# Keeping four groups' hidden layer of an FFN in SBUF, in a two-layer diffusion block on one core

## The chip, the cores and the metric

One NeuronCore of a Trainium2 chip runs the whole kernel as one program. The metric is the device time of one execution in microseconds, lower is better. Engines: PE (matrix multiply), DVE (vector), ACT (scalar and activation functions), POOL (GpSimd), SP (which here only issues DMAs).

## The reference

The input x has 128 sequences of 64 tokens of 256 features, 8192 tokens in all; cond is 128 x 256. Two layers each add to x:

```
hs = scan over 64 steps: gate = sigmoid(h @ Wh.T + z_t @ Wz.T + b); h = tanh(h*(1-alpha) + gate*z_t)   # z = x
xq = fake_quant(hs)                                  # one scale for the whole tensor, 8 bit
h  = silu(xq @ w_gate.T) * (xq @ w_up.T)             # 704 wide, quantised weights
x  = x + fake_quant(h) @ w_down.T                    # its scale needs max|h| over ALL tokens

# layer 1: adaptive layer norm, hyperbolic maps, attention of 16 heads inside each sequence, then an MLP
x2 = mobius_add(x, expmap(g_msa * attention(norm(x) * (1+sc_msa) + sh_msa)))
c  = mobius_add(x2, expmap(g_mlp * mlp(norm(x2) * (1+sc_mlp) + sh_mlp)))
out = x + fp6_block_quant(c) @ quantised(weight).T + bias
```

The maximum over all of h must be known before a single h can be quantised. So h has to be kept from the stage that makes it to the stage that uses it.

## The kernel before

The tokens stand as 64 tiles of 128 tokens, four tiles (512 tokens) to a group, 16 groups. The kernel has three stages.

**Scan** (until about 200 us). The 64 steps run one after another, with weight preparation in the gaps. `hsT` holds all steps in SBUF.

**h stage** (about 200 to 297 us). `hsT` is scaled to 8 bits into `xqT` in 16 blocks of 8 sequences (L493 to L507). Then for each group `tb`, `h_chunk` makes five tiles of h, 128 x 512 each; every second group adds a sixth tile with the last 64 columns of two groups. Each tile goes through ACT (silu), DVE or POOL (product `hv`), DVE (its maximum `am`), and a DMA stores it to DRAM (`h_d`, `hr_d`). At the end the maximum over everything gives the scale `cu`.

**Fused stage** (`fused`, from about 300 us). A loop over k from -5 to 18 runs a software pipeline. In iteration k stand, in program order:

- `tail(k)`: the Möbius sum of group k after attention, and of group k-3 after its MLP;
- `norms(k, ...)`: norm coefficients, `modulate`, the squares `un` of the norms, `su` from them, and the clip with `su`, for the MLP of group k and the attention of group k+5 together;
- `fp6(k-3)`: block quantisation, last matmul and the store of the result;
- `mlp(k)`, which ends in `tail_sums`;
- `attention(k+5)` in two pairs of tiles: `uT`, `qk`, `sq`, `nh`, `rh`, `comb`, `kT`, `e`, `raw`, the product into `u` (L1000), squares `tn`, `full`, `oT`, `av` (L1025), and then `tail_sums`;
- `front(k+6)`: loads h in pairs (`load_h`, `hl`), scales it to 8 bits with `cu` (`hb`, POOL), turns it to bf16 (`hq`), multiplies by `w_down` (`dn`), adds x (`xr`) and makes the statistics.

Iterations -5 to -1 have only attention work, 11 to 15 only the MLP, 16 to 18 only the last parts.

Sums of squares go through `square_sum`. ACT squares a tile into a scratch that nobody reads, and the accumulated sum is what counts. The scratch has one buffer for each tag, and the tag is made from the purpose and the engine: `u0`, `u1` for the norms (sums `un`), `o` for attention (`tn`), `ta`, `tm` for the tails (`ag`):

```
    def square_sum(e, tag, src, acc):

        junk = pl.tile([P, D], BF16, name="junk", tag=f"junk{tag}{e}", bufs=1)
```

Who is ahead of whom on an engine is decided when the program is built: a list scheduler takes the instructions by priority (program order, some chains raised by `first`), under the data dependencies and the order in which each tag's buffers are handed out. On the chip each engine executes its list in order. SBUF pools are stacks on the left and the right side; a tile of a pool that stands where another pool stood waits for the readers of that one.

Of the kernel before, what the change touches and what calls it, by code (L numbers as in the profile page):

```python
# [11 lines left out]
F32 = mybir.dt.float32  # L12
F32R = mybir.dt.float32r
BF16 = mybir.dt.bfloat16
I8 = mybir.dt.int8
F8 = mybir.dt.float8e4
# [6 lines left out]
P = 128  # L23
B, T, D = 128, 64, 256
# [17 lines left out]
GN = 4 * P  # L42
NG = NT // GN
AR = 8
TS = 4
CFG = {'rnd': 'S', 'ef': 8, 'fill': {'x1a': 'V', 'mod0': 'V'}, 'hold': [3, 0], 'mk': 2, 'raw': 1, 'mv': 6, 'xs': 3, 'la': 3, 'sb': 7, 'qks': 'GGGG', 'deq': 'VV', 'first': 1000, 'hb': 2, 'q_h': 'P', 'q_x1': 'P', 'q_xr': 'P', 'q_ot': 'P', 'q_out': 'P', 'q_ada': 'P', 'room': [[0.3, 0.3, 0.55], [0.5, 0.4, 0.2]], 'qv': 64, 'p1': 'GVGVGVGV', 'x1': 3, 'u1': 16, 'u2': 6, 'qkv': 2, 'sq': 1, 'uT1': 2, 'uT2': 2, 'qM': 2, 'kT': 2, 'e': 4, 'oT': 1, 'yT': 1, 'hq': 2, 'hl': 2, 'xr': 1, 'ot': 2, 'ada00': 2, 'ada02': 2, 'ada10': 2, 'ada12': 4, 'dn': 1, 'qk': 2, 'sc': 2, 'ao': 1, 'ml': 1, 'fp': 1, 'mod0': 'GGGV', 'mod1': 'VVVV', 'sqm0': 'SSSS', 'sqm1': 'SSSS', 'su0': 'VVVV', 'su1': 'VGVG', 'q8': 'GGGGGG', 'hqc': 'SSSVVV', 'qm': 'SSSS', 'x1a': 'GV', 'gate0': 'GGGG', 'gate1': 'GGGG', 'yb': 'GG', 'va': 'GGGG', 'sqt': 'SSSS', 'sqg': 'SSSS', 'sqo': 'SSVS', 'f2e': 'SSSS', 'early': 0, 'q8f': 'VVVVVV', 'hqf': 'SSSVVV', 'fl': 1, 'un': 2, 'jsu': 1, 'LA': 5, 'LM': 3, 'tl': 6, 'ord': 1, 'xt': 3, 'q_xt': 'P'}
GT = 4
NGR = NTILE // GT

LA, LM = CFG["LA"], CFG["LM"]  # L50
# [20 lines left out]
def tile_kernel(ctx, tc, a, out):  # L71
    nc = tc.nc
    V, S, G_, PE = nc.vector, nc.scalar, nc.gpsimd, nc.tensor
    dma = nc.sync.dma_start
# [65 lines left out]


    with ExitStack() as l0:
        fpool = l0.enter_context(tc.tile_pool(name="ffn0", bufs=1, side="right"))
        wgT = fpool.tile([P, 2, IF], BF16, name="wgT")
        wuT = fpool.tile([P, 2, IF], BF16, name="wuT")
        s_g = fpool.tile([P, 6], F32, name="s_g")
# [343 lines left out]
        fw = l0.enter_context(tc.tile_pool(name="fw", bufs=3))  # L490
        xp = hs_.enter_context(tc.tile_pool(name="xp", bufs=3))
        NBB = 8
        for b0 in range(0, B, NBB):  # L493
            for c in range(2):

                q8 = xp.tile([P, NBB, T], I8, name="q8", tag="q8")
                src = hsT[:, c, :, b0 : b0 + NBB].rearrange("p t b -> p b t")
                if b0 < CFG["qv"]:
                    V.tensor_scalar(q8, src, isx, None, ALU.mult)
                else:  # L500
                    G_.tensor_scalar(q8, src, isx, 0.0, ALU.mult, ALU.add)
                q8f = q8.rearrange("p b t -> p (b t)")
                dst = xqT[:, c, b0 * T : (b0 + NBB) * T]
                if c == 0:
                    V.tensor_copy(dst, q8f)
                else:
                    S.copy(dst, q8f)  # L507
        hs_.close()


        ps_a = l0.enter_context(tc.tile_pool(name="ps_a", bufs=3, space=PSUM))
# [1 line left out]

        cnt, silu = [0], []

        def h_chunk(pg, pu, j, at, dst):
            sil = fw.tile([P, GN], F32, name="sil", tag="sil")
            silu.append(S.activation(sil, pg, AF.Silu, scale=sgx[:, j : j + 1]))
            hv = fw.tile([P, GN], F32, name="hv", tag="hv", bufs=6)
            cnt[0] += 1  # L520
            if CFG["p1"][cnt[0] % 8] == "G":
                uv = fw.tile([P, GN], F32, name="uv", tag="uv")
                S.activation(uv, pu, AF.Copy, scale=sux[:, j : j + 1])
                G_.tensor_tensor(hv, uv, sil, ALU.mult)
            else:
                V.scalar_tensor_tensor(hv, pu, sux[:, j : j + 1], sil, ALU.mult, ALU.mult)  # L526
            V.tensor_reduce(am[:, j, at : at + 1], hv, AX.X, ALU.max, apply_absolute_value=True)  # L527
            dma(out=dst, in_=hv)

        V.memset(am, 0.0)  # L530
        for tb in range(NG):
            sl = slice(tb * GN, (tb + 1) * GN)
            for j in range(5):
                pg = ps_a.tile([P, GN], F32, name="pgate", tag="pgate")
                pu = ps_a.tile([P, GN], F32, name="pup", tag="pup")
                for ps, w in ((pg, wgT), (pu, wuT)):
                    for c in range(2):
                        PE.matmul(ps, lhsT=w[:, c, j * P : (j + 1) * P], rhs=xqT[:, c, sl],
                                  start=(c == 0), stop=(c == 1))
                h_chunk(pg, pu, j, tb, h_d[tb, j])  # L540
            if tb % 2:

                pg = ps_a.tile([P, GN], F32, name="pgate", tag="pgate")
                pu = ps_a.tile([P, GN], F32, name="pup", tag="pup")
                for ps, w in ((pg, wgT), (pu, wuT)):
                    for c in range(2):
                        for q in range(2):
                            s2 = slice((tb - 1 + q) * GN, (tb + q) * GN)
                            PE.matmul(ps[q * 64 : (q + 1) * 64], lhsT=w[:, c, 640:IF], rhs=xqT[:, c, s2],
                                      start=(c == 0), stop=(c == 1))  # L550
                h_chunk(pg, pu, 5, tb, hr_d[tb // 2])
        V.tensor_reduce(am1[:, 0:1], am, AX.XY, ALU.max)
        pmax(fpool, ps_t, am1[:, 1:2], am1[:, 0:1])
        sh = fpool.tile([P, 1], F32, name="sh")
# [7 lines left out]
def fused(ctx, tc, a, out_tok, x_tok, L):  # L562
# [8 lines left out]
    ada_d, h_d, hr_d, x1_d = (L[k] for k in ("ada_d", "h_d", "hr_d", "x1_d"))  # L571
    mx_scale, mx_round, ep, vas = (L[k] for k in ("mx_scale", "mx_round", "ep", "vas"))

    pl = ctx.enter_context(tc.tile_pool(name="fp", bufs=2))
    ps = ctx.enter_context(tc.tile_pool(name="fps", bufs=1, space=PSUM))
    one = ones[:, 0:1]
    len_pow = 4 * GT
# [10 lines left out]
    at = [0]  # L588
# [22 lines left out]
        return ps.tile([P, 512], F32, name=tag, tag=tag, bufs=CFG[tag])  # L611

    def big(tag, shape, dt=F32):
        return pl.tile(shape, dt, name=tag, tag=tag, bufs=CFG[tag])

    def square_sum(e, tag, src, acc):

        junk = pl.tile([P, D], BF16, name="junk", tag=f"junk{tag}{e}", bufs=1)
        if e == "S":
            S.activation(junk, src, AF.Square, accum_out=acc)  # L620
        else:
            V.scalar_tensor_tensor(junk, src, 1.0, src, ALU.mult, ALU.mult, accum_out=acc)

    def scale(e, dst, src, by):

        if e == "S":
            S.activation(dst, src, AF.Copy, scale=by)  # L627
        elif e == "V":
            V.tensor_scalar(dst, src, by, None, ALU.mult)  # L629
        else:  # L630
            G_.tensor_scalar(dst, src, by, 0.0, ALU.mult, ALU.add)  # L631
# [230 lines left out]

    def front(i):

        i0 = at[0] = i * GT
        x1 = x1s[i] = Pairs("x1")
        mv1 = get_mv(i - LA)[:, HA, :]
        for h2 in pairs:
            pr = i0 // 2 + h2
            early = pr < CFG["early"]  # L870
            grp = pr // 2
            hs_ = slice((grp % 2) * 64, (grp % 2) * 64 + 64)
            hl = hls.pop(0)
            hq = big("hq", [P, 6, 2 * P], BF16)
            q8 = big("hb", [P, 6, 2 * P], I8)

            for e, r, j in runs("q8f" if early else "q8", hs_):
                scale(e, q8[r, j, :], hl[r, j, :], cu[r])
            for e, r, j in runs("hqf" if early else "hqc", hs_):
                if e == "V":  # L880
                    V.tensor_copy(hq[r, j, :], q8[r, j, :])
                else:
                    S.copy(hq[r, j, :], q8[r, j, :])
            load_h(pr + CFG["hl"])
            xr = big("xr", [P, 2, D])
            move("xr", out=xr, in_=x_tok[:, i0 + 2 * h2 : i0 + 2 * h2 + 2, :])
            py = bank("dn")

            for i, j in [(i, j) for i in range(2) for j in range(5)] + [(0, 5), (1, 5)]:
                r = slice(0, P) if j < 5 else hs_  # L890
                PE.matmul(py[:, i * D : (i + 1) * D], lhsT=hq[r, j, i * P : (i + 1) * P], rhs=wdT[r, j, :],  # L891
                          start=(i == 0 and j == 0), stop=(j == 5), skip_group_check=True)
            V.tensor_tensor(x1.t[h2], two(py), bc_out(sdh, 2), ALU.mult)  # L893
            ENG[pick("x1a", h2)].tensor_tensor(x1.t[h2], x1.t[h2], xr, ALU.add)
            for g in (2 * h2, 2 * h2 + 1):
                stats(mv1[:, g, :], x1[g], 1)
            move("x1", out=x1_d[:, i0 + 2 * h2 : i0 + 2 * h2 + 2, :], in_=x1.t[h2])
# [172 lines left out]
    def fp6(i, av, s2):  # L1070
# [4 lines left out]
        for h2 in pairs:  # L1075
# [8 lines left out]
            V.reciprocal(mrc, msc)  # L1084
            V.tensor_tensor(of(mrc), of(mrc), bc_in(s2[:, hh], 8), ALU.mult)
            ENG[pick("yb", h2)].tensor_tensor(yb, yb, bc_in(mrc, 32), ALU.mult)
            y8 = pl.tile([P, 2 * D], F8, name="y8", tag="y8", bufs=2)
            if pick("rnd", h2) == "S":
                S.activation(y8, y, AF.Copy, bias=-(2.0 ** -27), scale=2.0 ** -6, saturate=False)
            else:  # L1090
# [78 lines left out]

    xss = {}  # L1170
    for pr in range(CFG["hl"]):
        load_h(pr)
    for i in range(CFG["fl"]):
        front(i)
    for k in range(-LA, NGR + LM):
        done = tail(k) if k >= 0 else None
        if done and CFG["ord"] == 0:
            fp6(k - LM, *done)
# [60 lines left out]
```

## Time and profile before

| | us |
|---|---|
| median of 3 runs | 1363.64 |
| lowest, highest | 1359.78, 1369.31 |
| profiled execution, its own time | 1362.89 |
| its span | 1361.0 |

| stage (stretch of the profile) | DVE busy of 34 us | PE busy | granted clock | DMA share |
|---|---|---|---|---|
| scan, 102 to 136 us | 20.44 | 34.00 | 1.00 | 0.23 |
| h stage, 238 to 272 us | 33.78 | 33.20 | 1.00 | 0.73 |
| start of the fused stage, 306 to 340 us | 22.63 | 13.08 | 0.50 | 0.99 |
| middle, 782 to 816 us | 31.62 | 29.38 | 0.85 | 0.32 |
| end, 1292 to 1326 us | 23.64 | 17.71 | 0.81 | 0.15 |

Times of the profile are counted from the start of the span. Busy time is the time in which an engine executes; "granted clock" is the share of full speed that PE was given; the DMA share is the mean busy share of the core's 16 DMA engines. Group rows give a source line, an engine, an operation, `out<-in` by the program's names, how often it ran, its busy time and mean ns, and the idle time just before with what ended it.

### The profile page before, as it was taken

The numbers are of one execution on the slowest core, as the hardware profiler recorded it, in microseconds if no ns is written. First come the engines' busy times: TensorE is split into PE (matmuls) and PEld (weight loads), VectorE is DVE, ScalarE is ACT, GpSimd is POOL, SyncE is SP. The second block draws the span as 40 slices with busy tenths as digits, with TensorE's granted clock in tenths as the row PEclk, the third lists the DMA queues.
The fourth block names the chain that finished last, engine by engine and source line by source line (L and its number), as shares of the span: only waits on it lengthen the run. The fifth ranks groups of instructions, "written<-read, shape, count | busy, mean of one in ns | idle before, by whom it ended". The sixth has DMA issues, their size and how long they took to land.

```text
span 1361.0 us, 23892 instructions
## 1 busy us (share of the span) xinstructions
PE 1103.2 (81%) x7404; PEld 758.7 (56%) x7404; DVE 1138.0 (84%) x3545; ACT 827.7 (61%) x2428; POOL 841.5 (62%) x1043
## 2 busy tenths in 40 slices
PE   6999967973698888899858988889988889777553
PEld 5766632332466566666636666566765666555332
DVE  5766679986779798978999899998999888897863
ACT  2455557971477777687756767656786568444331
POOL 3120128764689779687786867767767584656442
PEclk9999979985789888898878989598996898876786
DMA  7812105769625224432154531432414312142111
GB/s 234 301 55 67 43 16 212 280 255 289 196 85 161 85 79 136 147 124 74 54 155 151 172 100 39 148 107 81 125 44 132 105 59 71 59 125 85 62 47 46
DMA packets 119305, 163.65 MB, mean 120 GB/s; under 512 B 10885, under 2 KB 72074, under 8 KB 119178
## 3 DMA queue, kind: packets, MB, share of 16 engines
q1 hardware_dynamic: 119178, 162.13, 37.1%
q8 instruction: 58, 0.95, 0.3%
q14 instruction: 69, 0.57, 0.1%
HBM read 115.94 MB, written 46.14 MB: 119 GB/s over the span
## 4 chain that ended last, share of the span: by engine, by line
DVE 46%; PE 25%; POOL 12%; DMA 6%; issue 5%; ACT 5%; SPq 1%; DVEq 0%; POOLq 0%; ACTq 0%
PE pg L442 5%; DMA ada<-ada_d 3%; DVE u L808 3%; PE pg L423 3%; DVE am L527 2%; DVE u L735 2%; PE qk L926 2%; DVE u L629 2%; PE ml L1051 2%; DVE nh L931 2%; PE sc L977 2%; DVE bn L714 2%; DVE u L736 2%; DVE junk L754 2%; DVE hv L526 2%
## 5 line engine op out<-in xcount | busy, mean ns | idle before, releaser
L620 ACT ACTIVATE junk<-u 128x256 bf16<-128x256 f32 x432 | 183.5, 427 | 124.7 <-DVE u L736 33.0
L926 PE MATMUL qk<-wqkv,uT 128*128 128x512 f32 (+1 forms) x768 | 189.1, 386 | 8.0 <-DVE uT L917 4.1
L977 PE MATMUL sc<-qM,kT 64*64 64x256 f32 x1024 | 140.4, 452 | 21.7 <-ACT kT L967 19.7
L926 PEld LDWEIGHTS qk<-wqkv,uT 128*128 128x128 f32 x768 | 131.9, 206 | 29.6 <-DVE uT L917 7.0
L748 POOL TENSOR_TENSOR u<-u,ada 128x256 f32<-128x256 f32 x128 | 100.3, 786 | 65.2 <-ACT junk L620 60.3
L1051 PE MATMUL ml<-wm,uT 128*128 128x512 f32 (+1 forms) x384 | 117.8, 447 | 0.0
L994 PE MATMUL ao<-va,e 128*64 128x34 f32 x2048 | 94.9, 247 | 27.2 <-DVE u L1025 14.7
L994 PEld LDWEIGHTS ao<-va,e 128*64 128x64 f32 x2048 | 83.7, 162 | 55.9 <-DVE u L1025 17.3
L1051 PEld LDWEIGHTS ml<-wm,uT 128*128 128x128 f32 x384 | 82.8, 218 | 48.5 <-issue 19.6
L627 ACT ACTIVATE qM<-sc,mhead 128x256 f32<-128x256 f32 x256 | 101.8, 493 | 10.7 <-PE sc L92 10.7
L891 PE MATMUL dn<-wdT,hq 128*128 128x256 bf16 (+1 forms) x384 | 69.8, 329 | 42.6 <-DVE x L893 17.6
L977 PEld LDWEIGHTS sc<-qM,kT 64*64 64x64 f32 x1024 | 61.1, 153 | 68.7 <-ACT kT L967 28.3
L956 POOL TENSOR_TENSOR va<-qkv,comb 64x256 f32<-64x256 f32 x128 | 89.1, 696 | 12.6 <-PE ao L994 6.9
L620 ACT ACTIVATION_READ_ACCUMULATOR junk<-u 128x1 f32 x432 | 87.8, 203 | 0.0
L985 ACT ACTIVATE e<-sc 128x512 f32<-128x512 f32 x128 | 75.5, 607 | 15.6 <-PE sc L977 12.1
L442 PE MATMUL pg<-hsT,WT 128*128 128x128 f32 x504 | 76.5, 293 | 8.2 <-ACT hsT L454 7.7
L442 PEld LDWEIGHTS pg<-hsT,WT 128*128 128x128 f32 x504 | 66.2, 195 | 26.6 <-ACT hsT L454 23.4
L952 POOL TENSOR_TENSOR qkv<-qkv,comb 128x512 f32<-128x512 f32 x64 | 70.4, 1110 | 13.6 <-DVE dentc L791 3.5
L631 POOL TENSOR_SCALAR hb<-hl,cu 128x1280 int8<-128x1280 f32 x64 | 65.0, 1022 | 21.9 <-DMA hl<-h_d 15.4
L928 ACT COPY qkv<-qk 128x512 f32<-128x512 f32 (+1 forms) x128 | 61.2, 502 | 27.5 <-PE qk L926 27.0
L891 PEld LDWEIGHTS <-hq 128*128 128x128 bf16 (+1 forms) x384 | 38.7, 112 | 69.7 <-issue 38.1
L1105 PE MATMUL fp<-wfT,yT 128*128 128x256 f32 x256 | 77.0, 433 | 0.0
(289 smaller groups left out, 3184.1 us busy)
## 6 DMA issues: line engine op xcount, KB each, us to landing
ada<-ada_d SPq DMA_DIRECT2D x128, 256.0 KB, 3.5
h_d<-hv SPq DMA_DIRECT2D x80, 256.0 KB, 2.3
hl<-h_d SPq DMA_DIRECT2D x32, 640.0 KB, 4.6
ada<-ada_d SPq DMA_DIRECT2D x128, 128.0 KB, 2.4
xt<-in_xT_dram SPq DMA_DIRECT2D x16, 512.0 KB, 3.6
xr<-in_x_dram SPq DMA_DIRECT2D x32, 256.0 KB, 3.9
x_d<-x SPq DMA_DIRECT2D x32, 256.0 KB, 3.4
xt<-x_d SPq DMA_DIRECT2D x32, 256.0 KB, 2.8
```

The costliest lines, as they stand in the source:

```text
L442: lp = PE.matmul(pg[c][:, st], lhsT=WT[:, k, c * P : (c + 1) * P], rhs=hp[:, k, :], start=False, stop=False, skip_group_check=True)
L620: S.activation(junk, src, AF.Square, accum_out=acc)
L627: S.activation(dst, src, AF.Copy, scale=by)
L748: ENG[pick(f"gate{which}", g)].tensor_tensor(av, av, gb, ALU.mult)
L891: PE.matmul(py[:, i * D : (i + 1) * D], lhsT=hq[r, j, i * P : (i + 1) * P], rhs=wdT[r, j, :], start=(i == 0 and j == 0), stop=(j == 5), sk ...
L926: PE.matmul(pm[:, :n_], lhsT=uT[:, z, k, cs], rhs=wqkv[:, w, k, lo:hi], start=False, stop=(k == 1 and q == 2))
L956: ENG[pick("va", g)].tensor_tensor(va[r, :, s, 0:HD], qkv[r, xy, 512:768].rearrange("p (h d) -> p h d", d=HD), bc_in(comb[r, xy * 48 + 32 ...
L977: PE.matmul(sc[rr][s * T : (s + 1) * T, c * 256 : (c + 1) * 256].rearrange("p (v t) -> p v t", v=4), lhsT=kTs[xy][r, c, s * T : (s + 1) * ...
L985: S.activation(e.rearrange("p c v t -> p (c v t)"), sc[rr], AF.Exp, scale=1.0 / math.sqrt(HD))
L994: PE.matmul(pv[xy * T : (xy + 1) * T, hh], lhsT=E[2 * xy + hh // 4][:, c, hh % 4, :], rhs=vas[(2 * h2 + xy) % 4][:, c * 8 + hh], start=Tru ...
L1051: PE.matmul(pm[:, cs], lhsT=uT[:, z, k, i * P : (i + 1) * P], rhs=wm[:, w, k, cs], start=False, stop=(k == 1 and q == 2))
L1105: PE.matmul(o, lhsT=yT[:, 2 * i + c, :], rhs=wfT[:, c, :], start=False, stop=(c == 1))
```

## The change

Groups 0 to 3 keep their h in SBUF: `hk` (four tiles of 128 x 5 x 512 in f32, 10 KB a partition each) and `hkr` (two of 2 KB). They stand in a pool on the right side, opened where `hsT` was. Since that place is free only when `hsT` has been read, the h stage takes the groups in the order 4 to 15, 0 to 3. `front(0)` to `front(3)` read the kept tiles, and `load_h` begins with pair 8. At k = 0 the pool is closed, and a pool `late` takes its place. It holds eight kinds of tiles that are needed only from then on: `u2`, `uT2`, `yT`, `ot`, `ada10`, `ada12`, `xt`, `y8`. The scratch of `square_sum` has one tag for each engine instead of one for each purpose and engine.

```
+NK = 4
...
-        fpool = l0.enter_context(tc.tile_pool(name="ffn0", bufs=1, side="right"))
+        fpool = l0.enter_context(tc.tile_pool(name="ffn0", bufs=1))
...
-        for b0 in range(0, B, NBB):
+        order = [*range(NK, NG), *range(NK)]
+        for at, b0 in enumerate(NBB * n for n in order):
...
-                if b0 < CFG["qv"]:
+                if at * NBB < CFG["qv"]:
...
+        kept = ExitStack()
+        keep = kept.enter_context(tc.tile_pool(name="keep", bufs=1, side="right"))
+        hk = [keep.tile([P, 5, GN], F32, name=f"hk{i}") for i in range(NK)]
+        hkr = [keep.tile([P, 1, GN], F32, name=f"hkr{i}") for i in range(NK // 2)]
...
-        def h_chunk(pg, pu, j, at, dst):
+        def h_chunk(pg, pu, j, at, dst, hv=None):
...
-            hv = fw.tile([P, GN], F32, name="hv", tag="hv", bufs=6)
+            stays = hv is not None
+            if not stays:
+                hv = fw.tile([P, GN], F32, name="hv", tag="hv", bufs=6)
...
-            dma(out=dst, in_=hv)
+            if not stays:
+                dma(out=dst, in_=hv)
...
-        for tb in range(NG):
+        for tb in order:
...
-                h_chunk(pg, pu, j, tb, h_d[tb, j])
+                h_chunk(pg, pu, j, tb, h_d[tb, j], hk[tb][:, j, :] if tb < NK else None)
...
+    late = {"pool": None, "tags": {"u2", "uT2", "yT", "ot", "ada10", "ada12", "xt", "y8"}}
...
     def big(tag, shape, dt=F32):
-        return pl.tile(shape, dt, name=tag, tag=tag, bufs=CFG[tag])
+        return (late["pool"] if tag in late["tags"] else pl).tile(shape, dt, name=tag, tag=tag, bufs=CFG[tag])
...
-        junk = pl.tile([P, D], BF16, name="junk", tag=f"junk{tag}{e}", bufs=1)
+        junk = pl.tile([P, D], BF16, name="junk", tag=f"junk{e}", bufs=1)
...
-            hl = hls.pop(0)
+            hl = hls.pop(0) if gi >= NK else None
...
-                scale(e, q8[r, j, :], hl[r, j, :], cu[r])
+                if gi >= NK:
+                    src = hl[r, j, :]
+                else:
+                    src = hk[gi][r, j, ts] if j.start < 5 else hkr[gi // 2][r, :, ts]
+                scale(e, q8[r, j, :], src, cu[r])
...
-            load_h(pr + CFG["hl"])
+            if gi >= NK:
+                load_h(pr + CFG["hl"])
...
-        load_h(pr)
+        load_h(2 * NK + pr)
...
+        if k == 0:
+            kept.close()
+            late["pool"] = ctx.enter_context(tc.tile_pool(name="late", bufs=2, side="right"))
```

More of the change, by code (lines that the diff above doesn't have):

```diff
@@ L44 @@
 AR = 8
+NK = 4
 TS = 4
-CFG = {'rnd': 'S', 'ef': 8, 'fill': {'x1a': 'V', 'mod0': 'V'}, 'hold': [3, 0], 'mk': 2, 'raw': 1, 'mv': 6, 'xs': 3, 'la': 3, 'sb': 7, 'qks': 'GGGG', 'deq': 'VV', 'first': 1000, 'hb': 2, 'q_h': 'P', 'q_x1': 'P', 'q_xr': 'P', 'q_ot': 'P', 'q_out': 'P', 'q_ada': 'P', 'room': [[0.3, 0.3, 0.55], [0.5, 0.4, 0.2]], 'qv': 64, 'p1': 'GVGVGVGV', 'x1': 3, 'u1': 16, 'u2': 6, 'qkv': 2, 'sq': 1, 'uT1': 2, 'uT2': 2, 'qM': 2, 'kT': 2, 'e': 4, 'oT': 1, 'yT': 1, 'hq': 2, 'hl': 2, 'xr': 1, 'ot': 2, 'ada00': 2, 'ada02': 2, 'ada10': 2, 'ada12': 4, 'dn': 1, 'qk': 2, 'sc': 2, 'ao': 1, 'ml': 1, 'fp': 1, 'mod0': 'GGGV', 'mod1': 'VVVV', 'sqm0': 'SSSS', 'sqm1': 'SSSS', 'su0': 'VVVV', 'su1': 'VGVG', 'q8': 'GGGGGG', 'hqc': 'SSSVVV', 'qm': 'SSSS', 'x1a': 'GV', 'gate0': 'GGGG', 'gate1': 'GGGG', 'yb': 'GG', 'va': 'GGGG', 'sqt': 'SSSS', 'sqg': 'SSSS', 'sqo': 'SSVS', 'f2e': 'SSSS', 'early': 0, 'q8f': 'VVVVVV', 'hqf': 'SSSVVV', 'fl': 1, 'un': 2, 'jsu': 1, 'LA': 5, 'LM': 3, 'tl': 6, 'ord': 1, 'xt': 3, 'q_xt': 'P'}
+CFG = {'rnd': 'S', 'ef': 8, 'fill': {'x1a': 'V', 'mod0': 'V'}, 'hold': [3, 0], 'mk': 2, 'raw': 1, 'mv': 6, 'xs': 3, 'la': 3, 'sb': 7, 'qks': 'GGGG', 'deq': 'VV', 'first': 1000, 'hb': 2, 'q_h': 'P', 'q_x1': 'P', 'q_xr': 'P', 'q_ot': 'P', 'q_out': 'P', 'q_ada': 'P', 'room': [[0.3, 0.3, 0.55], [0.5, 0.4, 0.2]], 'qv': 64, 'p1': 'GVGVGVGV', 'x1': 3, 'u1': 16, 'u2': 6, 'qkv': 2, 'sq': 1, 'uT1': 2, 'uT2': 2, 'qM': 2, 'kT': 2, 'e': 4, 'oT': 1, 'yT': 1, 'hq': 2, 'hl': 2, 'xr': 1, 'ot': 2, 'ada00': 2, 'ada02': 2, 'ada10': 2, 'ada12': 4, 'dn': 1, 'qk': 2, 'sc': 2, 'ao': 1, 'ml': 1, 'fp': 1, 'mod0': 'GGGV', 'mod1': 'VVVV', 'sqm0': 'SSSS', 'sqm1': 'SSSS', 'su0': 'VVVV', 'su1': 'VGVG', 'q8': 'GGGGGG', 'hqc': 'SSSVVV', 'qm': 'SSSS', 'x1a': 'GV', 'gate0': 'GGGG', 'gate1': 'GGGG', 'yb': 'GG', 'va': 'GGGG', 'sqt': 'SSSS', 'sqg': 'SSSS', 'sqo': 'SSVS', 'f2e': 'SSSS', 'early': 0, 'q8f': 'VVVVVV', 'hqf': 'SSSVVV', 'fl': 1, 'un': 2, 'jsu': 1, 'LA': 5, 'LM': 3, 'tl': 6, 'ord': 1, 'xt': 3, 'y8': 2, 'q_xt': 'P'}
 GT = 4
@@ L550, in tile_kernel @@
                                       start=(c == 0), stop=(c == 1))
-                h_chunk(pg, pu, 5, tb, hr_d[tb // 2])
+                h_chunk(pg, pu, 5, tb, hr_d[tb // 2], hkr[tb // 2][:, 0, :] if tb < NK else None)
         V.tensor_reduce(am1[:, 0:1], am, AX.XY, ALU.max)
@@ L572, in fused @@
     mx_scale, mx_round, ep, vas = (L[k] for k in ("mx_scale", "mx_round", "ep", "vas"))
+    hk, hkr, kept = (L[k] for k in ("hk", "hkr", "kept"))
     pl = ctx.enter_context(tc.tile_pool(name="fp", bufs=2))
+    late = {"pool": None, "tags": {"u2", "uT2", "yT", "ot", "ada10", "ada12", "xt", "y8"}}
     ps = ctx.enter_context(tc.tile_pool(name="fps", bufs=1, space=PSUM))
@@ L863, in front @@
     def front(i):
-        i0 = at[0] = i * GT
+        gi, i0 = i, i * GT
+        at[0] = i0
         x1 = x1s[i] = Pairs("x1")
@@ L872, in front @@
             hs_ = slice((grp % 2) * 64, (grp % 2) * 64 + 64)
-            hl = hls.pop(0)
+            ts = slice(h2 * 2 * P, (h2 + 1) * 2 * P)
+            hl = hls.pop(0) if gi >= NK else None
             hq = big("hq", [P, 6, 2 * P], BF16)
@@ L1086, in fp6 @@
             ENG[pick("yb", h2)].tensor_tensor(yb, yb, bc_in(mrc, 32), ALU.mult)
-            y8 = pl.tile([P, 2 * D], F8, name="y8", tag="y8", bufs=2)
+            y8 = big("y8", [P, 2 * D], F8)
             if pick("rnd", h2) == "S":
```

## The prediction

> **What bounds the kernel now.** I read the page first, then the stretches of 34 us, the chain that ended last, the groups by line, and at last ACT's timeline and the order of the built program's instructions.
>
> ```profile
> PE 1103.2 (81%) x7404; PEld 758.7 (56%) x7404; DVE 1138.0 (84%) x3545; ACT 827.7 (61%) x2428; POOL 841.5 (62%) x1043
> ```
>
> No engine is full over the span. The stretches (PE, PEld, DVE, ACT, POOL busy us with counts, then granted clock, DMA share, GB/s) separate the stages: the second one below is the start of the fused stage, the third its middle.
>
> ```profile
> 238.00:272.00 34.00, 33.20 (x152) 12.94 (x150) 33.78 (x55) 32.71 (x57) 27.10 (x22) 1.00 0.73 278
> 306.00:340.00 34.00, 13.08 (x57) 7.28 (x57) 22.63 (x70) 6.47 (x15) 15.81 (x17) 0.50 0.99 289
> ...
> 816.00:850.00 34.00, 30.36 (x208) 21.98 (x205) 32.32 (x110) 25.79 (x75) 26.34 (x31) 1.00 0.11 35
> ```
>
> The h stage (about 206 to 297) is full of DVE work. The fused stage begins with a DMA-bound stretch, 99% busy with PE at 13 us of 34. Later DVE is nearly full. Before 306 us DVE was busy 234.3 us (the sum of the first nine stretches), so the fused stage holds 903.7 us of DVE work, 56.5 us for each of the 16 groups. From the end of group 0's last `av` (L1025, 437 us) to group 15's (1237 us) the pace is 53.3 us a group. So the middle runs at DVE's pace.
>
> It can do so only because several groups are in flight. ACT's timeline shows it:
>
> ```profile
> 354.30 0.59 ACT L916 CAST uT<-qk 128x512 fp32r<-128x512 f32 x1 [0.58 <-PE qk L92]
> 354.78 0.42 ACT L620 ACTIVATE junk<-u 128x256 bf16<-128x256 f32 x1
> ...
> 388.75 0.41 ACT L620 ACTIVATE junk<-u 128x256 bf16<-128x256 f32 x1
> ...
> 417.33 0.58 ACT L1016 COPY oT<-ao 128x512 f32<-128x512 f32 x1
> ```
>
> The first row starts group 0's attention, the last is its output transpose. By the instruction order, the `junk<-u` squares at 354.78 and 388.75 are the norm squares of groups 1 and 2. They go out while group 0 is still in attention. I took every group's time from that first `uT` to its last `av`: 83 us for group 0, 110 to 163 us for the others. At a pace of 53 that is more than two groups at once.
>
> **The change part by part.** *The removed transfers.* Groups 0 to 3 write no h (20 stores to h_d and 2 to hr_d) and their 8 pairs load none (8 hl<-h_d, 8 hl<-hr_d), 5.8 MB each way.
>
> ```profile
> h_d<-hv SPq DMA_DIRECT2D x80, 256.0 KB, 2.3
> hl<-h_d SPq DMA_DIRECT2D x32, 640.0 KB, 4.6
> ```
>
> The stores lie under 33.8 of 34 us of DVE in the h stage, so they are worth 0; without that cover, one store of 2.3 us at its end. The loads fall into the DMA-bound stretch and are on the path:
>
> ```profile
> 302.41 6.88 DMA hl<-h_d
> 309.31 7.23 DMA xr<-in_x_dram
> ```
>
> That xr would take its median of 3.9 us, which gives 3.3 us. At most POOL's whole wait on hl (15.4 us in its group `hb<-hl`) goes too: 18.7 us. A loss is possible as well, on SP's queue: the ada loads of group 0's last two tiles (331.25 us in the profile) now stand behind the fifth xr and five loads into the late pool. The late pool opens after 8 pairs of `hb` scales, 8 x (1.42 + 0.62) = 16.3 us from 300, so at about 317. The fifth xr waits for the fourth block's sum (L894), which came at 334.2 us, held up by hl loads; if it came no sooner, the start would be 3 us later. So -3 to 18.7 us. I take 5, nearest the xr row.
>
> *Moved work.* The order of the 16 blocks in the h stage changes, and not their count: PE, DVE, ACT and POOL have as many instructions as before, SP 38 fewer. `hb` reads the kept tile in the same shape, 1.42 us. These cost 0; their cover is that the operations are the same. Eight kinds of tiles (`u2`, `xt`, `ot` and others) open only when the kept tiles are read. Their first use that matters is the first combine (L808, 477 us); cover 150 us, so 0.
>
> *The one scratch name.* In square_sum the tag `junk{tag}{e}` becomes `junk{e}`. The scratch has one buffer, and buffers of a tag are handed out in program order. With one tag, ACT's squares of all kinds stand in program order: norm squares (un), then the MLP's (ag), the attention's (tn), its tail's (ag), then the next iteration's un. The instruction order says so. ACT's squares formed 156 runs of one kind before, starting un 1 to 12, tn 1 to 2, un 13 to 14. Now they form 69: un 1 to 4, tn 1 to 3, ag 1 to 8, un 5 to 8, and so on to the end, without an exception. ACT executes in order. Group i+1 gets no norm square, so no scale, no clip, no attention, before group i's last gate square. No instruction is added; the overlap of groups is taken away. Behind a waiting square on ACT stand the copies of `qk` and `uT` on which PE and DVE wait.
>
> So one iteration lasts as long as its chain. I split an attention pair at events of the timeline and took, over all 32 pairs, the smallest and the tenth percentile of each segment (us):
>
> - first `uT` to second `sq`: 8.2 and 13.2; to `rh`: 2.4 and 3.4; to `comb`: 2.2 and 3.1; to second `kT`: 7.1 and 10.6; to last `e`: 7.1 and 8.8; to second `raw`: 5.8 and 7.5; to L1000: 1.5 and 1.9. Sum 34.3 and 48.5.
> - second pair behind the first at L1000: 9.7 and 9.9; to `full`: 4.1 and 4.2; to the group's last `av`: 8.7 and 9.0; then square 0.63, gate 0.79, square 0.63: 2.0.
> - ahead of it: four un squares 4 x 0.63 = 2.5, `su` 0.27 + 1.72 + 0.32 = 2.3, two clips 1.0, four transposes 1.2: 7.0. With the MLP in the iteration, four more squares and four more clips of 0.52: 11.6.
>
> That makes 65.8 to 80.6 us where only attention runs, and 70.4 to 85.2 us where the MLP runs beside it. The minima were never all met by one pair (the quickest took 46.7, not 34.3), but the tenths come from a crowded kernel. I take 70 and 80. Iterations k = -5 to -1 are of the first kind, k = 0 to 10 of the second. In k = 11 to 15 only the MLP is left: from `sur` at 1300.84 to the last gate square at 1332.1 is 31 us,
>
> ```profile
> 1300.84 0.32 POOL L666 TENSOR_SCALAR sur<-sur 128x8 f32<-128x8 f32 x1
> ```
>
> and with squares and `su` 36; the largest distance of two `sur` there is 50. I take 39. From 1332 to the end at 1361 is 29.
>
> **The sum.** Start of the first un square 331.3 - 5 = 326; 5 x 70 = 350; 11 x 80 = 880; 5 x 39 = 195; 29. Span 1780. The profiled run took 1362.89 for its 1361.0, and the median of the runs is 0.75 above it: 1783 us. With the low ends (313 + 329 + 774 + 180 + 29) it is 1628, with the high ends (334 + 403 + 937 + 250 + 29) 1956.
>
> A rule speaks against this. The Trainium skill, "Perfetto Trace Analysis", section "Identifying the Most-Contended Engine", says that the engine with the highest occupancy is the bottleneck. Here that is DVE, 84%, and its work is unchanged; by the rule the time would stay near 1361. I hold the timeline against it: occupancy is the bound only while enough groups are in flight to fill it. A second rule speaks for more: "TensorE: Matmul & The Clock Gate", Part 1, has PE's clock fall to half when PE is little busy. The trace agrees where PE was busy 13.08 of 34 us (clock 0.50, against 1.00 at 30.36). By the rule the sum would move to its upper end.
>
> **The rivals.** *DVE still sets the middle.* Iterations of about 60 us (56.5 of DVE and a little), with only the start and the end serial: 326 + 5 x 66 + 11 x 60 + 180 + 29 = 1525, so 1528. For it: DVE's work of other stages (tail, fp6, front) needs no ACT square ahead of it and can fill the gaps. Against: the chain's minima alone are 70. *The chain at crowded prices.* If queues stay as long as now, a pair's medians hold: 80.7 + 16.7 + 10.5 + 12.8 + 2 + 11.6 = 134 against 80; half way, 107, gives 1780 + 11 x 27 = 2077. Against: those medians come from more than two groups in flight. *The change as its words say.* ACT's order costs nothing, the loads are gone: 1361 - 18.7 = 1342, so 1345. It wins if the serial chain is no longer than DVE's 56.5 us a group; the sum of smallest segments, 65.8, is already longer. Lost order with fewer loads could also cancel within 1%, about what a measurement of this kernel can tell from no change.
>
> **How the numbers follow.** The forecast has 0.65, the DVE-paced case 0.18, the crowded one 0.09, the last 0.05, a near-cancelling 0.03. Range 1530 to 1950: the forecast's own bounds, drawn out to the DVE-paced case. Faster 0.05, same 0.03, slower 0.92.
>
> **What would show it.** In the profile after: DVE below 70%, granted clock lower, the first un square near 326, `sur` once per iteration at 65 to 85 us, L1025 of a group always ahead of the next group's L916, ACT's long waits at `junk<-u`. It is wrong if DVE stays above 80% in the middle, or if two groups' attention overlap on PE.

## The result and the profile after

The changed kernel takes 1838.37 us (median of 6 runs, 1837.43 to 1840.22), the kernel before 1365.11 us beside it (6 runs, 1359.78 to 1372.28). The ratio is 1.347, with a 95% interval of 1.3438 to 1.3502. The profiled execution took 1838.6 us, its span is 1836.8 us. The prediction said 1783 us, 1530 to 1950. In the kernel after, the source lines have moved: `junk<-u` L620 is L635, `uT` L916 is L938, `oT` L1016 is L1038, `av` L1025 is L1047, the product L1000 is L1022, `sur` L666 is L681.

The first line of the page, busy time of each engine with its share of the span:

```profile
PE 1291.0 (70%) x7370; PEld 865.3 (47%) x7404; DVE 1100.4 (60%) x3545; ACT 877.2 (48%) x2428; POOL 815.2 (44%) x1043
```

The instruction counts are those of before (some PE records are missing), but DVE has fallen from 84% to 60% of the span. No engine is full. The chain that ended last, by engine, says it too:

```profile
PE 21%; POOL 21%; DVE 16%; ACT 11%; issue 9%; DMA 3%; POOLq 0%; SPq 0%; ACTq 0%; DVEq 0%
```

The shares add up to 81%, since this chain is followed back only to about 350 us. The same line before:

```profile
DVE 46%; PE 25%; POOL 12%; DMA 6%; issue 5%; ACT 5%; SPq 1%; DVEq 0%; POOLq 0%; ACTq 0%
```

DVE's 46% have become 16%. Now no engine holds more than 21%: the chain walks through four engines in turn, which is what one dependent chain looks like.

Two stretches of the kernel after, in the columns of the prediction: the start of the fused stage and its middle. The last row is the same middle before.

```profile
306.00:340.00 34.00, 16.36 (x70) 8.59 (x69) 27.73 (x87) 7.88 (x18) 24.63 (x48) 0.50 0.62 177
800.00:900.00 100.00, 67.30 (x405) 46.95 (x408) 59.42 (x196) 49.73 (x144) 53.15 (x67) 0.67 0.39 115
...
800.00:900.00 100.00, 83.57 (x599) 58.15 (x595) 94.56 (x320) 68.14 (x207) 73.62 (x90) 0.81 0.26 81
```

At the start the DMA share has fallen from 0.99 to 0.62, so the loads are gone as the change says. In the middle DVE works 59.42 of 100 us, against 94.56 before. The DMA issues show the same removal, 20 stores and 8 loads of pairs fewer:

```profile
h_d<-hv SPq DMA_DIRECT2D x60, 256.0 KB, 2.2
hl<-h_d SPq DMA_DIRECT2D x24, 640.0 KB, 5.3
```

ACT's timeline over group 0's attention (start, length, then line, operation and tiles, and in brackets the idle time before it):

```profile
347.11 0.59 ACT L938 CAST uT<-qk 128x512 fp32r<-128x512 f32 x1 [0.22 <-PE qk L93]
...
426.95 0.58 ACT L1038 COPY oT<-ao 128x512 f32<-128x512 f32 x1 [1.00 <-PE ao L93]
...
435.20 0.42 ACT L635 ACTIVATE junk<-u 128x256 bf16<-128x256 f32 x1 [0.83 <-POOL u L763]
...
435.74 0.42 ACT L635 ACTIVATE junk<-u 128x256 bf16<-128x256 f32 x1
```

The first row starts group 0's attention. The third is the last gate square of its tail, at 435.20. The fourth is the first norm square of group 1. Before, the norm squares of groups 1 and 2 stood at 354.78 and 388.75, inside group 0's attention; now the first comes 0.54 us after the last gate square. The next group's `uT` follows at 443.35, and group 0's last two `av` (L1047) started at 431.40. So it goes for all 15 groups that follow another: no `uT` of a group ahead of the last `av` of the group before.

`sur` (L681) comes once per iteration and shows the pace:

```profile
342.08 0.29 POOL L681 TENSOR_SCALAR sur<-sur 128x8 f32<-128x8 f32 x1
441.06 0.27 POOL L681 TENSOR_SCALAR sur<-sur 128x8 f32<-128x8 f32 x1
514.26 0.26 POOL L681 TENSOR_SCALAR sur<-sur 128x8 f32<-128x8 f32 x1
...
727.65 0.26 POOL L681 TENSOR_SCALAR sur<-sur 128x8 f32<-128x8 f32 x1
811.92 0.27 POOL L681 TENSOR_SCALAR sur<-sur 128x8 f32<-128x8 f32 x1
...
1628.19 0.27 POOL L681 TENSOR_SCALAR sur<-sur 128x8 f32<-128x8 f32 x1
1664.27 0.27 POOL L681 TENSOR_SCALAR sur<-sur 128x8 f32<-128x8 f32 x1
...
1778.36 0.27 POOL L681 TENSOR_SCALAR sur<-sur 128x8 f32<-128x8 f32 x1
```

Five iterations of attention alone take (727.65 - 342.08) / 5 = 77.1 us, the first of them 99.0. Eleven with attention and MLP take (1628.19 - 727.65) / 11 = 81.9. Four with the MLP alone take (1778.36 - 1628.19) / 4 = 37.5.

Last, the group of the squares on the page, before and after (busy, mean ns, then ACT's idle time before them and what ended most of it):

```profile
L620 ACT ACTIVATE junk<-u 128x256 bf16<-128x256 f32 x432 | 183.5, 427 | 124.7 <-DVE u L736 33.0
...
L635 ACT ACTIVATE junk<-u 128x256 bf16<-128x256 f32 x432 | 180.6, 418 | 236.4 <-POOL u L763 110.2
```

432 squares of 418 ns, hardly shorter than before (427). The idle time ahead of them has grown from 124.7 to 236.4 us. The largest part, 110.2 us, ends with POOL's gate (L763), the product that stands between the two squares of each tile of a tail.

### The profile page after: what moved, and what is told of

Its sections match the earlier page's. It is cut to its first block, busy times and chain, and to the rows that moved or that the text cites. A ratio compares the mean times of both kernels' runs of the same rounds, so it can differ in the third digit from the quotient of the medians.

```text
span 1836.8 us, 23979 instructions
## 1 busy us (share of the span) xinstructions
PE 1291.0 (70%) x7370; PEld 865.3 (47%) x7404; DVE 1100.4 (60%) x3545; ACT 877.2 (48%) x2428; POOL 815.2 (44%) x1043
## 3 DMA queue, kind: packets, MB, share of 16 engines
q1 hardware_dynamic: 110122, 150.60, 26.4%
## 4 chain that ended last, share of the span: by engine, by line
PE 21%; POOL 21%; DVE 16%; ACT 11%; issue 9%; DMA 3%; POOLq 0%; SPq 0%; ACTq 0%; DVEq 0%
PE qk L948 7%; PE ml L1073 4%; ACT junk L635 4%; POOL u L763 4%; POOL r L666 3%; DMA ada<-ada_d 3%; DVE u L823 2%; PE sc L999 2%; ACT qM L642 2%; POOL va L978 2%; POOL sur L666 2%; POOL qkv L974 2%; PE dn L913 1%; PE ao L1016 1%; POOL u L1108 1%
## 5 line engine op out<-in xcount | busy, mean ns | idle before, releaser
L635 ACT ACTIVATE junk<-u 128x256 bf16<-128x256 f32 x432 | 180.6, 418 | 236.4 <-POOL u L763 110.2
L999 PE MATMUL sc<-qM,kT 64*64 64x256 f32 x1024 | 194.1, 600 | 54.4 <-ACT kT L989 33.6
L763 POOL TENSOR_TENSOR u<-u,ada 128x256 f32<-128x256 f32 x128 | 95.7, 747 | 144.8 <-ACT junk L635 143.9
L1016 PEld LDWEIGHTS ao<-va,e 128*64 128x64 f32 x2048 | 117.6, 210 | 77.0 <-issue 35.5
L948 PEld LDWEIGHTS qk<-wqkv,uT 128*128 128x128 f32 x768 | 131.2, 206 | 46.8 <-ACT uT L938 27.9
L1016 PE MATMUL ao<-va,e 128*64 128x34 f32 x2048 | 133.2, 290 | 11.9 <-ACT raw L1019 8.0
L999 PEld LDWEIGHTS sc<-qM,kT 64*64 64x64 f32 x1024 | 81.3, 200 | 116.2 <-ACT kT L989 46.4
L953 DVE TENSOR_REDUCE nh<-sq 128x48 f32<-128x768 f32 x64 | 60.9, 952 | 119.4 <-ACT sq L952 119.4
L93 PE MATMUL ml<-ident,u 128*128 128x128 f32 x128 | 31.1, 378 | 143.8 <-DVE u L644 92.2
L1043 PE MATMUL ao<-wo,oT 128*128 128x256 f32 x256 | 98.1, 550 | 15.7 <-ACT oT L1038 15.6
L93 PEld LDWEIGHTS ml<-ident,u 128*128 128x128 f32 x128 | 19.4, 182 | 155.0 <-DVE u L644 98.2
L769 DVE CUSTOM_DVE_ANT_0 junk<-u,u 128x256 bf16<-128x256 f32 x64 | 30.7, 479 | 99.1 <-POOL u L763 99.0
L1043 PEld LDWEIGHTS ao<-wo,oT 128*128 128x128 f32 x256 | 67.7, 278 | 37.1 <-ACT oT L1038 24.3
```

What stands on the lines that cost most here:

```text
L763: ENG[pick(f"gate{which}", g)].tensor_tensor(av, av, gb, ALU.mult)
L948: PE.matmul(pm[:, :n_], lhsT=uT[:, z, k, cs], rhs=wqkv[:, w, k, lo:hi], start=False, stop=(k == 1 and q == 2))
L999: PE.matmul(sc[rr][s * T : (s + 1) * T, c * 256 : (c + 1) * 256].rearrange("p (v t) -> p v t", v=4), lhsT=kTs[xy][r, c, s * T : (s + 1) * ...
L1016: PE.matmul(pv[xy * T : (xy + 1) * T, hh], lhsT=E[2 * xy + hh // 4][:, c, hh % 4, :], rhs=vas[(2 * h2 + xy) % 4][:, c * 8 + hh], start=Tru ...
L1043: PE.matmul(pm[:, i * D : (i + 1) * D], lhsT=oT[:, 2 * i + c, :], rhs=wo[:, c, :], start=(c == 0), stop=(c == 1))
```

## The experiments

**The theory.** With one scratch tag the squares of all kinds go out in program order. The next group's norm squares then stand behind the last gate square of the group before, and each iteration is one chain. **The rivals:** the rest of the change (the order of the blocks, the kept tiles, the late pool) causes the slowdown; or the number of scratch buffers does; or squares that wait on ACT cost time in general, in whatever order.

All diffs are against the kernel named in the heading. "Before" ratios are against runs of the kernel before on the same chip.

**1. The kernel before, with the one tag alone.**

```
-        junk = pl.tile([P, D], BF16, name="junk", tag=f"junk{tag}{e}", bufs=1)
+        junk = pl.tile([P, D], BF16, name="junk", tag=f"junk{e}", bufs=1)
```

> The kernel before with one edit: the scratch tag of square_sum is one for each engine, as in the changed kernel. h of all groups goes through DRAM as before, no kept tiles, no late pool. My theory (the one scratch tag puts all squares of ACT in program order, so iterations run one after another): 1820 to 1870 us, sur once in about 80 us in the middle, DVE near 60% busy. Rival (the kept tiles and the late pool, or the fewer loads with another order of the groups, make it slow): within 2% of before, 1345 to 1390.

Measured: 1826.98 us (1824.77 to 1832.54, 4 runs), ratio 1.3377 (1.3332 to 1.3423).

```profile
PE 1291.6 (71%) x7404; PEld 862.3 (47%) x7404; DVE 1104.1 (60%) x3545; ACT 879.2 (48%) x2428; POOL 815.8 (45%) x1043
```

The busy times are, within 0.4%, those of the changed kernel. One line of code makes 463 of the 473 us. The changed kernel is 1838.37 - 1826.98 = 11 us above it; since experiment 3, which keeps nothing either, takes 1838 us too, these 11 us can't be put down to the kept groups.

**2. The changed kernel, norm squares apart from the rest** (three tags: norm squares on ACT, other squares on ACT, other squares on DVE).

```
-        junk = pl.tile([P, D], BF16, name="junk", tag=f"junk{e}", bufs=1)
+        junk = pl.tile([P, D], BF16, name="junk", tag=f"junk{tag[0] == 'u'}{e}", bufs=1)
```

> The changed kernel with one edit: three scratch tags (norm squares on ACT, other squares on ACT, squares on DVE) instead of two, which is all that the room allows. Norm squares may go out ahead of an earlier group's tail squares again. My theory: near before or somewhat faster, 1320 to 1390 us, with two and more groups in flight. Rival (kept tiles and late pool cost it): still above 1600.

Measured: 1381.65 us (1378.9 to 1387.5, 4 runs), ratio 1.0126 (1.0087 to 1.0166). One more tag, 512 bytes a partition, takes away 457 of the 473 us. ACT's squares again start with 12 of the norms in the built program, as before. The time is 1.3% above the kernel before, so "near before" holds and "somewhat faster" doesn't. The first norm square came at 327.90, near the 326 of the prediction.

**3. The kernel before, one tag with five buffers on ACT.**

```
-        junk = pl.tile([P, D], BF16, name="junk", tag=f"junk{tag}{e}", bufs=1)
+        junk = pl.tile([P, D], BF16, name="junk", tag=f"junk{e}", bufs=5 if e == "S" else 1)
```

> The kernel before with one scratch tag for each engine, but five buffers for ACT's, so that there is as much scratch as with the old tags. My theory (not the number of buffers but the order in which one tag's buffers are handed out binds): as slow as with one buffer, 1800 to 1870 us. Rival (a lack of scratch buffers makes the squares wait): within 3% of before.

Measured: 1837.99 us (one run). Five buffers are no faster than one. In the built program ACT's squares form the same 69 runs of one kind. So what costs the time is not that a square waits for a scratch that is still in use. It is that buffers of a tag are handed out in program order, however many there are, so a later square isn't placed ahead of an earlier one.

**4. Keeping two groups, with the old tags** (against the changed kernel).

```
-NK = 4
+NK = 2
...
-        junk = pl.tile([P, D], BF16, name="junk", tag=f"junk{e}", bufs=1)
+        junk = pl.tile([P, D], BF16, name="junk", tag=f"junk{tag}{e}", bufs=1)
```

> The changed kernel with two kept groups instead of four (NK = 2), which leaves room for all of the old scratch tags. My theory: the order of ACT's squares is free again; what is left of the change is 11 stores and 8 loads fewer at the start of the fused stage, worth 0 to 15 us: 1335 to 1375 us. Rival (the kept tiles and the late pool cost it): half of the way to 1838, about 1600.

Measured: 1358.71 us (1355.59 to 1364.61, 10 runs), ratio 0.9967 (0.9942 to 0.9992). First norm square at 328.90.

**5. Keeping four groups, with the old tags; scratches that are needed late stand in the late pool** (against the changed kernel). With every old tag in the left pool the `fp` pool lacks room: it needs 111.78 KB a partition, and 110.44 KB are left. This is why moving or merging some scratch is part of keeping four groups.

```
-        junk = pl.tile([P, D], BF16, name="junk", tag=f"junk{e}", bufs=1)
+        junk = (late["pool"] if tag in ("u1", "tm") else pl).tile([P, D], BF16, name="junk", tag=f"junk{tag}{e}", bufs=1)
...
-        junk = pl.tile([P, D], BF16, name="junk", tag=f"junkx{tag}", bufs=1)
+        junk = late["pool"].tile([P, D], BF16, name="junk", tag=f"junkx{tag}", bufs=1)
...
-                junk3 = pl.tile([P, D], BF16, name="junk3", tag="junkz", bufs=1)
+                junk3 = late["pool"].tile([P, D], BF16, name="junk3", tag="junkz", bufs=1)
```

> The changed kernel with four kept groups and every old scratch tag of square_sum. The room comes from the late pool: scratch that is used only from k = 0 on (the MLP's squares, the products with x) stands there. My theory: the order of ACT's squares is free again and the loads stay removed, 1335 to 1375 us, at most 20 us below before, since POOL waited 15.4 us for hl loads in all. Rival (kept tiles and late pool cost something of their own): 1380 us like the version with three tags.

Measured: 1358.85 us (1353.06 to 1367.2, 12 runs), ratio 0.996 (0.9932 to 0.9989), so 0.1 to 0.7% faster than the kernel before. This and the two kept groups are the fastest versions here, and not told apart. The busy times and the start of its fused stage:

```profile
PE 1088.1 (80%) x7404; PEld 746.5 (55%) x7404; DVE 1149.1 (85%) x3545; ACT 826.7 (61%) x2428; POOL 843.8 (62%) x1043
```

```profile
306.00:340.00 34.00, 14.15 (x60) 7.58 (x59) 27.27 (x89) 7.89 (x18) 24.04 (x38) 0.50 0.66 191
```

DVE is back at 85%. At the start the DMA share is 0.66, near the 0.62 of the changed kernel, and the first norm square came at 326.5, 4.7 us earlier than before. That is the gain that the prediction gave the removed transfers. Whether the 5 us by which the whole kernel is faster are these same 5 us was not shown.

**6. The kernel before, with the three tags of experiment 2.** The edit is that of experiment 2.

> The kernel before with the three scratch tags (norm squares on ACT, others on ACT, DVE), nothing kept. It tells whether the 18 us by which the changed kernel with three tags is above before come from the tags or from the kept groups. My theory (the attention's squares and the tails' are still in program order among themselves, so it is the tags): 1370 to 1395 us. Rival (it is the kept groups and the late pool): 1355 to 1370 us.

Measured: 1400.49 us (1397.56 to 1402.52, 4 runs), ratio 1.0263 (1.0219 to 1.0307). That is 5 us above the expected range, and far from the rival's. The weaker tie among the squares still costs 37 us without kept groups, and experiment 2, with kept groups, is 19 us below it. With all the old tags the difference is 5 us (experiment 5 against the kernel before), with one tag it has the other sign, 11 us (the changed kernel against experiment 1). Each of these edits also gives a new order of instructions, so what of the 19 and the 11 us is due to the kept groups was not shown.

**7 and 8. One more step in the chain:** the power on POOL that makes `su` (1.65 us in experiment 7) runs a second time, with the same result, in the changed kernel and in the kernel before.

```
+        if tag == "su":
+            rsqrt(t, q, tag)
```

> The changed kernel with one suspected step of the chain doubled: the power on POOL that makes su (1.7 us) is executed a second time with the same result, 21 times in all. My theory (each iteration is one chain, and su stands in it): 21 x 1.7 = 36 us more than the changed kernel's 1838, 1865 to 1885 us. Rival (an engine's work sets the pace; POOL is 44% busy): 1830 to 1850 us.

> The same doubled step in the kernel before. My theory (there groups overlap and the step is covered in the middle): at most 12 us more, 1360 to 1376 us, from the start and the end alone. Rival (su is on the path of every iteration there as well): 36 us more, 1400 us.

Measured: 1859.11 us (1851.81 to 1866.58, ratio 1.3617), 20.7 us more than the changed kernel; and 1377.56 us (1372.65 to 1379.14, ratio 1.0091), some 14 us more than the kernel before. Both expectations missed, 36 being too much for the first and 12 too little for the second; by the total the test hardly tells the theories apart. The two traces of the changed kernel, without and with the second power, show where a part of it went. Over the last ten groups, from the last `oT` of one group to `uT` of the next the distance grew from 20.5 to 22.1 us: the step is in the chain, for its full 1.6 us. But from there to the group's own last `oT` it shrank from 62.0 to 61.0 us; that engines had other work out of the way meanwhile is likely, and was not shown. The four distances of `sur` with the MLP alone grew by far more than the step, from 150.2 to 165.4 us together, and that was not explained. So a step's length is not what it adds to the time: other work beside the chain can give part of it back, or more can come on top.

**9 and 10. Which tie closes the chain:** the changed kernel with the tails' squares apart, and with attention's squares apart.

```
-        junk = pl.tile([P, D], BF16, name="junk", tag=f"junk{e}", bufs=1)
+        junk = pl.tile([P, D], BF16, name="junk", tag=f"junk{tag[0] == 't'}{e}", bufs=1)
```

In the second, 'o' stands for 't'.

> The changed kernel, with a scratch tag of its own for the tails' squares (ag); norm squares (un) and attention's squares (tn) still share one. In the built order ACT then has un of the next iteration ahead of the tails' squares: un 1 to 4, tn 1 to 3, un 5 to 8, ag 1 to 8, and so on. Theory (each iteration is one chain, closed by the order in which the one scratch is handed out): the chain of an iteration now ends at the last tn and no more at the last gate square. By the profile of the changed kernel that cuts off 5.6 us (product to full), 8.7 (full to the last av) and 2 (two squares and the gate), some 15 to 16 us in each of 16 iterations, so 240 to 260 us less: 1580 to 1600, and 1540 to 1680 with what other work gives back; the distance of two sur in the middle 64 to 72 us, DVE 67 to 72% busy. Rival (what costs the time is that squares of all kinds block ACT in general, not one closed chain): un and tn still follow one another in program order, so most of the loss stays, 1750 to 1840. Second rival (un only has to be free of the tails' squares): 1380 to 1420, as with the three tags.

> The changed kernel, with a scratch tag of its own for attention's squares (tn); norm squares and the tails' squares still share one. The order of ACT's squares is the same as in the changed kernel, without exception: since the gate squares come after tn by their data, tying un to them ties everything. Theory: 1838 us within 1%. Rival (a count of tags is what matters, as two names instead of one): 1400 to 1600, like the other kernel of this call.

Measured: 1634.8 us (1632.8 to 1637.06, 4 runs), ratio 1.1992 (1.1939 to 1.2045); and 1842.07 us (1841.33 to 1842.82, 2 runs), ratio 1.3518 (1.3441 to 1.3595). The second has one more name and ACT's order unchanged, and it gains nothing. The first lies inside the expected 1540 to 1680, above its point of 1580 to 1600. Its busy times, and ACT's timeline around the end of group 0's attention:

```profile
PE 1273.1 (78%) x7370; PEld 852.0 (52%) x7404; DVE 1094.1 (67%) x3545; ACT 862.9 (53%) x2428; POOL 815.6 (50%) x1043
```

```profile
418.90 0.42 ACT L635 ACTIVATE junk<-u 128x256 bf16<-128x256 f32 x1 [2.07 <-DVE u L1022]
...
419.44 0.42 ACT L635 ACTIVATE junk<-u 128x256 bf16<-128x256 f32 x1
...
427.77 0.42 ACT L635 ACTIVATE junk<-u 128x256 bf16<-128x256 f32 x1 [1.13 <-DVE u L1047]
...
435.07 0.59 ACT L938 CAST uT<-qk 128x512 fp32r<-128x512 f32 x1 [0.19 <-PE qk L93]
```

The first row is attention's last square, released by the product L1022. The first norm square of group 1 stands right behind it, at 419.44, and the tail's first square (released by `av`, L1047) only after that. In the changed kernel it was the other way round. Mean distances, groups 1 to 5 and 6 to 15 (us):

| | last L1022 to next `su` | `su` to `uT` | `uT` to last L1022 | sum |
|---|---|---|---|---|
| changed kernel | 22.1; 27.9 | 2.5; 3.3 | 48.4; 51.3 | 73.0; 82.5 |
| tails' squares apart | 7.9; 11.2 | 3.6; 4.0 | 51.3; 56.0 | 62.8; 71.2 |

The cut part became 14.2 and 16.7 us shorter, where 15 to 16 were expected: the chain ran through `full`, `av` and the gate squares, at that price. The other parts became 4.0 and 5.4 us longer; the tail of the last group now runs beside the next group's attention, which is the likely reason. Net 10.2 and 11.3 us an iteration.

## Why the prediction was right, and where its sizes were off

The direction and the mechanism held. Experiment 1 shows the cause alone, 3 that it is the order and not the room, 2, 9 and 10 which part of the order.

**Each iteration one chain.** Term by term, on the span:

| term | predicted | measured |
|---|---|---|
| first un square | 326 | 330.1 |
| iterations -5 to -1 | 5 x 70 | 5 x 77.1 |
| iterations 0 to 10 | 11 x 80 | 11 x 81.9 |
| iterations 11 to 15 and the end | 5 x 39 + 29 = 224 | 12 (first un square to `sur`) + 4 x 37.5 + 58.5 = 221 |
| span | 1780 | 1836.8 |

The sum was 57 us short: some 4 from the start, 36 from the first five iterations, 21 from the eleven, less 3 at the end.

**The term furthest off is 5 x 70.** The four later iterations took 71.7 on average (from 441.06 to 727.65), near the 70. The first took 99.0, so 29 of the 36 us are in the first iteration alone. The prediction gave it the price of the others. Most of the excess lies between `uT` and the last product L1022: 69.4 us for group 0, 48.4 on average for groups 1 to 5. Group 0's attention has the fronts that still fill the pipeline beside it: from its first `uT` to its last `av` POOL works 60.93 of 85.17 us and DVE 58.01, for group 2 (516.54 to 579.83) 28.08 and 33.88 of 63.29. That this work delays it is likely, and no run tested it. In experiment 1, with nothing kept, the first iteration took 90.2 us; there `uT` to L1000, the same product, took 48.3, and the excess came behind it (35.8 us to the next `sur`, 24.6 in the changed kernel). So the first iteration is dear in both, in different places.

**Inside an iteration** the split into segments was sound, although no pair met all the minima before. The smallest from `uT` to the product was 46.7 us before. In the changed kernel it is 34.0, the sum of the predicted minima being 34.3; the median is 41.0, between the minima and the 48.5 of the tenths. So a pair does go faster when groups run one after another, and the "crowded" rival, with its 134 us an iteration, fell. In the middle the attention part took 51.3, and the tail with the next norms 31.2 (27.9 + 3.3). By the prediction's terms those were 80 - 26.4 = 53.6 and 26.4 (4.1 + 8.7 + 2.0 + 11.6). The stretch from the product to the next `uT` was sized at its minima and is the one that was too small, by 4.8 us; the attention part was 2.3 us too long. That the 80 came within 2 us of the 81.9 is in part luck: the two errors partly cancel, and 80 was a choice between 70.4 and 85.2.

**The removed transfers: 5 us predicted, 1.1 measured** (331.25 to 330.14). The stretch that the prediction priced does hold: from `cu` (its reciprocal at 302.25, before at 299.54 us) to the first norm square it is 27.9 us against 31.7. In all seven traces that keep groups it is 27.1 to 28.2 us, in all five that keep none 30.9 to 31.7. So keeping groups saves some 4 us there. The rest was lost ahead of it: `cu` came 2.7 us later. The prediction gave the h stage no such change. Over the kernels here, one of them with nothing of this change in it (experiment 8, 302.73), `cu` comes between 299.4 and 303.4 us. Why it spreads was not settled.

**The DVE-paced rival** (1528) fell: DVE worked 59.42 of 100 us in the middle. Even experiment 9, with one tie fewer, has DVE at no more than 67% of the span. **The rival by the words of the change** (1345) needed ACT's order to cost nothing. With that order free, 1358.85 was measured: faster than before, as that rival says, but by 5 us and not by 18.7. Read as a bound on the time, as the prediction read it, the rule of the Trainium skill on occupancy ("Perfetto Trace Analysis", "Identifying the Most-Contended Engine") would have kept the time near 1361. Experiment 1 leaves every engine its instructions and measures a ratio of 1.3377, so here the measurement decides against that reading: in this kernel the busiest engine set the pace only while several groups were in flight.

**The signs named** came in: DVE at 60% (below 70), a lower granted clock (0.729 against 0.86 over the span), `sur` once per iteration (67 to 85 us, apart from the first), no two groups' attention overlapping. ACT's idle time ahead of `junk<-u` nearly doubled. The first un square was 4 us off.

## What to carry to other kernels

A scratch tile that nobody reads still orders work: uses that share one tag are built in program order, and more buffers don't help (1363, 1827 and 1838 us for separate tags, one tag, one tag with five buffers). Before merging scratches to save room, compare each engine's order of instructions, and keep apart above all the uses that start a software-pipelined iteration from all that come later in it. With the norm squares apart from all others the changed kernel took 1382 us, with the tails' squares apart 1635, with attention's apart 1842. Or move late scratches into a pool that opens late; that saved the room at no cost that was measured here (1358.85 us).

When overlap is lost, time each link of the chain from the trace, and price the first iteration by itself: it runs beside the filling of the pipeline, and here it took 99.0 us where the next four took 71.7.

## What was not expected of the hardware

PE's busy time rose from 1103.2 to 1291.0 us although its instructions are the same. Busy time times the granted clock over the span is 1103.2 x 0.86 = 949, 1291.0 x 0.729 = 941 and, in experiment 9, 1273.1 x 0.747 = 951 us. In all twelve kernels here the product lies between 929 and 958. That fits the same work done at a lower clock. The group that lengthened most in total shows it, before and after (mean ns in the column after the busy time):

```profile
L977 PE MATMUL sc<-qM,kT 64*64 64x256 f32 x1024 | 140.4, 452 | 21.7 <-ACT kT L967 19.7
...
L999 PE MATMUL sc<-qM,kT 64*64 64x256 f32 x1024 | 194.1, 600 | 54.4 <-ACT kT L989 33.6
```

These matmuls went from 452 to 600 ns on average. Most large groups lengthened, though not all: the `qk` products took 386 ns before and 376 after. So a chain that leaves PE idle makes most of its own matmuls slower here. "TensorE: Matmul & The Clock Gate", Part 1, of the Trainium skill says that the clock falls when PE is little busy. The trace agrees in direction: in the stretch of 800 to 900 us PE was busy 83.57 us at a clock of 0.81 before, and 67.30 us at 0.67 after. But the busy share alone doesn't tell the clock: experiments 6 and 9 both have PE at 78% of the span, with 0.867 and 0.747. Matmuls that take longer also count as busy for longer. How many of the 473 us are due to the clock was not separated from the rest.
